# Constant tiles set once, and a value copy that takes only the changing columns, in a fused attention and mixture-of-experts block

## The chip, the cores and the metric

The kernel runs on one core of one Trainium2 chip. Its engines each work through a queue of their own: TensorE (PE in the profile; PEld is its weight load), VectorE (DVE), ScalarE (ACT), GpSimd (POOL) and SyncE (SP), which here only issues DMAs. The metric is device time in microseconds, the median of several runs; lower is better. All data are fp32.

## The reference

One transformer block on a sequence of 2048 rows of 256 numbers: attention with 16 heads of width 16 (keys and values come from a latent of 64), a residual and a layer norm, then 16 experts with the two best per row, a shared expert, a residual and a layer norm.

```python
q = (x @ Wq).reshape(B, S, HEADS, HEAD_DIM).transpose(0, 2, 1, 3)
c_kv = x @ Wkv_down
k = (c_kv @ Wk_up) ...        # 12 of 16 numbers of q and k are rotated (rope)
v = (c_kv @ Wv_up) ...
scores = einsum('bhqd,bhkd->bhqk', qf, kf) * scale       # causal
weights = softmax(scores)
out = einsum('bhqk,bhkd->bhqd', weights, v)
x = layernorm(x + out)
scores = softmax(t @ gate_w.T); weights, indices = top_k(scores, 2)
y = sum over experts e of swiglu(t, w1[e], w3[e], w2[e]) * w_e
x = layernorm(x + y + swiglu(t, sw1, sw3, sw2))
```

## The kernel before

**Layout.** Heads are handled four at a time, in four groups `g`. Each head takes 32 columns (PAD): 16 numbers of the head, then column 16 (ONE), then columns that are zero or copies. The 2048 rows are cut into four chunks `c` of 512 and, for keys and values, into 16 blocks of 128. All four heads of a group share a tile of 128 partitions or 128 columns, and their matmuls use 32 rows or columns of TensorE each.

**Attention.** `prologue(c)` transposes a chunk of x and makes the latent. `project_k`, `project_q` and `project_v` make a group's keys, queries and values; `project_k` ends in a GpSimd sum (L428). Scores are computed twice. A `Maxima` step multiplies queries by keys (tile m) and VectorE takes the row maxima (L485 on the diagonal, L490 elsewhere). When all maxima of `(g, c)` are there, `negated` (L492) reduces them and writes the negative into column ONE of a tile `nm` of 128x512 that is zero elsewhere, and `shift` (L500), two steps later, transposes `nm` on TensorE (tile pn) and adds it to the queries (L508), so that the keys' column of ones carries the negative maximum into the second product. A `Weighted` step multiplies keys by those queries (tile s), ScalarE takes the exponential (L535, tile p), GpSimd masks the diagonal (L539), and TensorE multiplies by the values (tile av). Column ONE of the values is 1, so it collects the sum of the weights. ScalarE copies av out (L566, `more`) and GpSimd adds it to `avs` (L567); in steps without a `Maxima` part VectorE adds it directly (L563).

**The values.** `project_v(g, c)` makes 4 products of 128x128 in two PSUM banks. ScalarE copies each bank's 256 columns into a tile `v` (L453, two copies), out of a pool of six buffers, and GpSimd then sets column ONE of each of 16 head parts to 1 (L457). The padded value weights are zero outside the 16 columns of each head, so the copied padding is zero. There are 16 calls of `project_v` and 16 of `negated`.

**Order.** A list of 180 steps, each a `Maxima` part, a `Weighted` part or both, is written out for all groups, and projections, transposes and ends are put at chosen steps (`put`). TensorE's instructions keep that order. The other engines' queues are ordered by the framework, which takes the instruction of highest priority among those it reckons to be ready by its own estimates of durations; it also places the semaphore waits. `nm` has one buffer: its GpSimd memset (L494) must wait until TensorE has transposed the contents before.

**The rest.** After attention come the norm, the choice of experts, a scatter of rows by GpSimd's indirect DMAs (L278), the blocks of 128 rows per expert, an indirect scatter back (L931), and the combination.

The lines that matter here:

```python
            v = kv.tile([P, CH], F32, tag="v", bufs=6, name=f"v{g}_{c}")
            for a in range(2):
                nc.scalar.copy(
                    v.rearrange("p (b a m) -> p b a m", a=2, m=P)[:, :, a, :],
                    pv[a][:, : 2 * P].rearrange("p (b m) -> p b m", m=P),
                )
            nc.gpsimd.memset(v.rearrange("p (h d) -> p h d", d=PAD)[:, :, ONE : ONE + 1], 1.0)
```

Of the kernel before, what the change touches and what calls it, by code (L numbers as in the profile page):

```python
# [1 line left out]

# [8 lines left out]
F32 = mybir.dt.float32  # L11
# [6 lines left out]
P = 128  # L18
S, E = 2048, 256
H, HD, LAT = 16, 16, 64  # L20
NOPE, RD = 4, 12
G = 4
PAD = 32
LOW = HD + NOPE
ONE = HD
CH = 512
# [21 lines left out]
def block_kernel(  # L48
# [14 lines left out]
    nc = tc.nc  # L63
# [78 lines left out]
    def matmul(*args, **kw):  # L142
        pe(nc.tensor.matmul, *args, **kw)
# [142 lines left out]
    with ExitStack() as att:  # L286
        ap1 = att.enter_context(tc.tile_pool(name="ap1", bufs=1))
        kv = att.enter_context(tc.tile_pool(name="kv", bufs=8))
        wk1 = att.enter_context(tc.tile_pool(name="wk1", bufs=1))
# [102 lines left out]
            out=xg[NEXP * S :, :], in_=blank  # L392
        )

        qs, ks, vs, qa, pm, avs = {}, {}, {}, {}, {}, {}

        def bank(name):
            return ps_sc.tile([P, CH], F32, tag="sc", name=name)
# [41 lines left out]
        def project_v(g, c):  # L440

            pv = [bank(f"pv{g}_{c}_{a}") for a in range(2)]
            for b in range(4):
                a = b % 2
                r = slice(a * LAT, (a + 1) * LAT)
                matmul(
                    pv[a][:, (b // 2) * P : (b // 2 + 1) * P],
                    lhsT=ckv[c][r, b * P : (b + 1) * P],
                    rhs=wvs[r, g * P : (g + 1) * P], start=True, stop=True,
                )  # L450
            v = kv.tile([P, CH], F32, tag="v", bufs=6, name=f"v{g}_{c}")
            for a in range(2):
                nc.scalar.copy(  # L453
                    v.rearrange("p (b a m) -> p b a m", a=2, m=P)[:, :, a, :],
                    pv[a][:, : 2 * P].rearrange("p (b m) -> p b m", m=P),
                )
            nc.gpsimd.memset(v.rearrange("p (h d) -> p h d", d=PAD)[:, :, ONE : ONE + 1], 1.0)  # L457
            vs[g, c] = v

        class Maxima:  # L460
# [29 lines left out]
                        nc.vector.tensor_reduce(to, ps, AX.X, ALU.max)  # L490

        def negated(g, c):  # L492
            nm = wk1.tile([P, 4, 4, PAD], F32, tag="nm", name=f"nm{g}_{c}")
            nc.gpsimd.memset(nm, 0.0)  # L494
            nc.vector.tensor_reduce(
                nm[:, :, :, ONE], pm[g, c][:, :, :, : c + 1], AX.X, ALU.max, negate=True
            )
            return nm
# [96 lines left out]
        def whole_m(g, c):  # L595
            return [(g, c, t, kc) for t in range(4) for kc in range(c)]
# [31 lines left out]
        m = whole_m(1, 3)  # L628
# [5 lines left out]
        for g in range(1, G):  # L634
# [9 lines left out]
            else:  # L644
                m = whole_m(g + 1, 3)
# [25 lines left out]
        for step, what, c in (  # L671
            (1, project_k, 1), (1, project_q, 1), (3, prologue, 2), (4, project_v, 0),
            (6, project_k, 2), (7, prologue, 3), (9, project_v, 1), (9, project_q, 2),
            (14, project_k, 3), (17, project_q, 3), (19, project_v, 2), (32, project_v, 3),
        ):
            if what is prologue:
                put(step, what, c)
            else:
                put(step, what, 0, c)
        for g in range(1, G):  # L680
            i = m_first[g, NCH - 1]
# [5 lines left out]
        for (g, c), i in m_last.items():  # L687
            def late(i=i, g=g, c=c):
                nm = negated(g, c)
                put(i + 2, shift, g, c, nm)  # L690
            put(i, late)
            assert i + 3 <= s_first[g, c]
# [23 lines left out]
        while step < len(steps) or prior or at:  # L716
            m, s = steps[step] if step < len(steps) else (None, None)
            m = m and Maxima(*m)
# [376 lines left out]
```

## Time and profile before

| | |
|---|---|
| Median of 3 runs | 812.88 us (811.92 to 813.79) |
| Profiled execution | 803.1 us, its span 801.1 us |
| Mean granted TensorE clock | 0.993 |
| Attention | about 0 to 594 us of the span |
| Experts and combination | about 594 to 801 us |

The page of the profile gives busy time by engine; the groups give it by line and shape, with the idle time of the engine just before and who ended it; a question about one line or tile tells who waited for it; the timeline lists instructions in order of time. The profiled execution is 1.2% shorter than the median of the timed runs, so differences are worked out in its microseconds and then put on the median.

### The profile page before, as it was taken

What the parts mean: (1) busy time and instruction counts of PE and PEld (TensorE: products, weight loads), DVE (VectorE), ACT (ScalarE), POOL (GpSimd) and SP (SyncE); (2) the same over time, 40 slices, a digit from 0 to 9 for tenths busy, and PEclk for the clock granted to TensorE, in tenths of its full rate; (3) what the DMA queues carried; (4) which work ended last, traced back from release to release, by engine and by line L of the source; (5) the groups of instructions that cost most, each with busy time, mean ns of one, the idle gap of its engine ahead of it and who ended that gap; (6) DMA issues with size and microseconds to landing.
All of it is one profiled execution on the core that took longest, in us unless ns stands there. A gap on an engine that the chain in (4) does not pass through costs nothing. (4 is left out here: it accounts for less than half of the span.)

```text
span 801.1 us, 14999 instructions
## 1 busy us (share of the span) xinstructions
PE 771.5 (96%) x5086; PEld 361.3 (45%) x5086; DVE 547.1 (68%) x1489; ACT 445.0 (56%) x997; POOL 323.0 (40%) x557
## 2 busy tenths in 40 slices
PE   7999999999999999999999999999989899999985
PEld 3443433444333344543334453444336466666543
DVE  2768888887687887777788678788775433333276
ACT  1143646377775786766688668875742033333345
POOL 2032524434355454635455454461661333333300
PEclk9999999999999999999999999999999999999998
DMA  5469999991000000001000000000225322222172
GB/s 147 130 174 327 310 301 304 294 301 54 2 1 1 1 2 1 2 19 37 1 2 2 1 2 2 1 2 2 80 84 141 107 80 86 82 86 70 37 230 85
DMA packets 67378, 71.88 MB, mean 90 GB/s; under 512 B 4736, under 2 KB 61539, under 8 KB 67302
## 3 DMA queue, kind: packets, MB, share of 16 engines
q1 hardware_dynamic: 62286, 61.77, 27.7%
q0 software_dynamic: 3552, 8.43, 3.0%
q10 hardware_dynamic: 1464, 0.72, 0.4%
q8 instruction: 41, 0.67, 0.4%
q14 instruction: 35, 0.29, 0.1%
HBM read 26.44 MB, written 45.78 MB: 90 GB/s over the span
## 5 line engine op out<-in xcount | busy, mean ns | idle before, releaser
L535 ACT ACTIVATE p<-s 128x512 f32<-128x512 f32 (+3 forms) x640 | 292.6, 540 | 128.2 <-PE m L140 79.0
L140 PE MATMUL m<-k,q 32*128 32x512 f32 (+3 forms) x1280 | 303.9, 566 | 0.8 <-DVE rot L423 0.5
L140 PE MATMUL s<-qa,k 32*128 32x512 f32 (+3 forms) x1280 | 279.4, 556 | 1.8 <-DVE avs L563 0.7
L490 DVE TENSOR_REDUCE pm<-m 128x1 f32<-128x512 f32 x384 | 237.5, 681 | 44.4 <-PE m L140 44.0
L567 POOL TENSOR_TENSOR avs<-avs,more 128x512 f32<-128x512 f32 (+3 forms) x125 | 136.7, 1094 | 167.3 <-ACT more L566 163.8
L140 PEld LDWEIGHTS s<-qa,k 32*128 32x128 f32 x1280 | 107.1, 184 | 117.6 <-ACT p L535 67.6
L140 PE MATMUL av<-p,v 128*32 128x512 f32 (+3 forms) x1280 | 154.2, 540 | 1.9 <-DVE base L244 1.2
L140 PEld LDWEIGHTS m<-k,q 32*128 32x128 f32 x1280 | 122.7, 184 | 44.5 <-issue 11.9
L485 DVE CUSTOM_DVE_ANT_0 m<-m,qmask 128x512 f32<-128x512 f32 (+3 forms) x256 | 118.3, 521 | 29.1 <-PE m L140 26.1
L566 ACT COPY more<-av 128x512 f32<-128x512 f32 (+3 forms) x125 | 65.6, 525 | 38.3 <-PE av L140 30.4
L539 POOL TENSOR_SCALAR_AFFINE_SELECT p<-p 128x128 f32<-128x128 f32 x256 | 70.5, 297 | 38.2 <-ACT p L535 36.4
L931 POOL DMA_INDIRECT yg<-yb,to x42 | 41.4, 985 | 88.2 <-ACT yb L923 44.1
L140 PEld LDWEIGHTS av<-p,v 128*32 128x32 f32 x1280 | 27.1, 108 | 104.1 <-ACT p L535 54.2
L140 PE MATMUL ph<-w,xbT 128*128 x168 | 60.3, 482 | 2.4 <-DVE xbT L884 1.7
L903 DVE TENSOR_TENSOR rh<-ru,ph 128x176 f32<-128x176 f32 x42 | 14.2, 338 | 53.7 <-ACT ru L901 53.7
L140 PE MATMUL h<-xT,cs 128*128 128x512 f32 (+1 forms) x96 | 43.6, 599 | 4.9 <-DVE sh L794 2.0
L901 ACT ACTIVATE ru<-ph 128x176 f32<-128x176 f32 x42 | 13.3, 318 | 59.3 <-PE ph L140 59.3
L140 PE MATMUL py<-w2r,hT 88*128 x168 | 43.4, 380 | 0.7 <-ACT hT L910 0.7
L278 POOL DMA_INDIRECT xg<-xr,slot x32 | 31.1, 971 | 31.1 <-issue 19.8
L140 PEld LDWEIGHTS ph<-w,xbT 128*128 128x128 f32 x168 | 28.5, 189 | 20.8 <-issue 11.6
L428 POOL TENSOR_TENSOR k<-rot 128x512 f32<-128x512 f32 x16 | 20.3, 1267 | 42.5 <-DVE rot L426 42.5
L140 PEld LDWEIGHTS py<-w2r,hT 88*128 88x128 f32 x168 | 31.7, 189 | 12.0 <-ACT hT L910 1.2
(147 smaller groups left out, 633.3 us busy)
## 6 DMA issues: line engine op xcount, KB each, us to landing
xg<-hot SPq DMA_DIRECT2D x16, 2064.0 KB
w<-in_w_dram SPq DMA_DIRECT2D x4, 1408.0 KB
xb<-xg SPq DMA_DIRECT2D x42, 129.0 KB
got<-yg SPq DMA_DIRECT2D x8, 512.0 KB
w2r<-in_w_dram SPq DMA_DIRECT2D x2, 1408.0 KB
xr<-in_x_dram SPq DMA_DIRECT2D x4, 512.0 KB
out_dram<-o SPq DMA_DIRECT2D x8, 256.0 KB
cs<-in_rope_dram SPq DMA_DIRECT2D x16, 80.0 KB
```

What stands on the lines that cost most here:

```text
L140: tc.keep_in_program_order(op(*args, **kw))
L278: put = nc.gpsimd.indirect_dma_start(out=xg[:, :], out_offset=bass.IndirectOffsetOnAxis(ap=slot[:, j, i : i + 1], axis=0), in_=xr[c][:, t, ...
L428: nc.gpsimd.tensor_tensor(ks[g, c], tmp[:, 0, :], tmp[:, 1, :], ALU.add)
L485: nc.vector.tensor_tensor_reduce(out=ps[:, :n], in0=ps[:, :n], in1=qmask[:, CH - n :], scale=1.0, scalar=3.0 * NEG, op0=ALU.add, op1=ALU.m ...
L490: nc.vector.tensor_reduce(to, ps, AX.X, ALU.max)
L535: nc.scalar.activation(pr[:, n0:], ps[:, n0:], AF.Exp, scale=SCALE)
L539: nc.gpsimd.affine_select(out=diag, in_=diag, pattern=[[1, P]], base=0, channel_multiplier=-1, compare_op=ALU.is_ge, fill=0.0,)
L566: nc.scalar.copy(more[:, n0:], pv[:, n0:])
L567: nc.gpsimd.tensor_tensor(to, to, more[:, n0:], ALU.add)
L901: nc.scalar.activation(u, ph[:, :INTER], AF.Silu)
L903: nc.vector.tensor_tensor(us[b], u, ph[:, INTER:], ALU.mult)
L931: nc.gpsimd.indirect_dma_start(out=yg[:, :], out_offset=bass.IndirectOffsetOnAxis(ap=to[:, 0:1], axis=0), in_=yb, in_offset=None, bounds_c ...
```

## The change

The tiles for the negated maxima (two, instead of a pool of one buffer) and for the values (six, as many as the pool had) are made once, before the steps begin. GpSimd fills all eight with zeros, and sets column ONE of each of 16 head parts in the six value tiles to 1: 14 memsets, written after the loads and before the first projection. `negated` and `project_v` then take them in a fixed turn. The memset in `negated` and the one in `project_v` go, and ScalarE's two copies in `project_v` take 16 of every 32 columns, 128 elements in each partition instead of 256. TensorE's instructions and their order stay.

```diff
+        turn_nm, turn_v = itertools.count(), itertools.count()
+
+        minus = [ap1.tile([P, 4, 4, PAD], F32, tag=f"nm{i}", name=f"nm{i}") for i in range(2)]
+        room_v = [ap1.tile([P, CH], F32, tag=f"v{i}", name=f"v{i}") for i in range(6)]
+        for t in minus + room_v:
+            nc.gpsimd.memset(t, 0.0)
+        for v in room_v:
+            nc.gpsimd.memset(
+                v.rearrange("p (h d) -> p h d", d=PAD)[:, :, ONE : ONE + 1], 1.0
+            )
...
-            v = kv.tile([P, CH], F32, tag="v", bufs=6, name=f"v{g}_{c}")
+            v = room_v[next(turn_v) % len(room_v)]
             for a in range(2):
                 nc.scalar.copy(
-                    v.rearrange("p (b a m) -> p b a m", a=2, m=P)[:, :, a, :],
-                    pv[a][:, : 2 * P].rearrange("p (b m) -> p b m", m=P),
-                )
-            nc.gpsimd.memset(v.rearrange("p (h d) -> p h d", d=PAD)[:, :, ONE : ONE + 1], 1.0)
+                    v.rearrange("p (b a h d) -> p b a h d", a=2, h=4, d=PAD)[:, :, a, :, :HD],
+                    pv[a][:, : 2 * P].rearrange("p (b h d) -> p b h d", h=4, d=PAD)[:, :, :, :HD],
+                )
...
-            nm = wk1.tile([P, 4, 4, PAD], F32, tag="nm", name=f"nm{g}_{c}")
-            nc.gpsimd.memset(nm, 0.0)
+            nm = minus[next(turn_nm) % 2]
             nc.vector.tensor_reduce(
                 nm[:, :, :, ONE], pm[g, c][:, :, :, : c + 1], AX.X, ALU.max, negate=True
             )
```

## The prediction, made before the result was known

> **What bounds the kernel now.** First the page's busy times, then stretches of time, to see whether one engine alone sets the pace of attention. (Columns of the stretches: length, then busy us and instructions of PE, PEld, DVE, ACT, POOL; granted clock; DMA.)
>
> ```profile
> PE 771.5 (96%) x5086; PEld 361.3 (45%) x5086; DVE 547.1 (68%) x1489; ACT 445.0 (56%) x997; POOL 323.0 (40%) x557
> 260.00:310.00 50.00, 50.00 (x402) 19.68 (x400) 40.01 (x91) 38.69 (x81) 23.91 (x37) 1.00 0.01 1
> 460.00:510.00 50.00, 49.98 (x433) 22.78 (x430) 39.81 (x110) 37.49 (x89) 25.09 (x53) 1.00 0.01 1
> ```
>
> In mid-attention TensorE is never idle at a full clock, DVE is busy for 80%, ACT for 75%, POOL for 50%. A full PE row isn't PE at its peak, so the waits matter: PE's weight loads wait longest for ACT's exponentials (67.6 and 54.2 us in all). The pace is a loop of PE, ACT and DVE through the eight PSUM banks; POOL has room. The change takes work from POOL and a little from ACT, so I ask of each removed instruction who waited for it. The questions about lines 494, 457 and 453 answer (summary rows, then "its engine idle until", then "who waited for it"):
>
> ```profile
> L494 POOL MEMSET nm<- x16: 525/526/529, 8.0 to 530.0; 128x512 f32 x16
>   PE pn L140: 12.9, 10
> L457 POOL MEMSET v<- x16: 123/126/131, 35.2 to 479.8; 128x16 f32 x16
>   ACT v L453: 18.1, 7
>   PEld av L140: 0.8, 1
> L453 ACT COPY v<-pv x32: 372/377/440, 34.5 to 479.3; 128x256 f32<-128x256 f32 x32
>   PEld s L140: 1.9, 4
>   PEld m L140: 1.2, 6
> ```
>
> **Part 1, POOL's 32 memsets.** They are 16 x 0.526 + 16 x 0.126 = 10.4 us of POOL, and POOL stood 12.9 + 18.1 us at their heads with everything behind them held. Were that on the path it would be 41 us. The timeline of POOL says it isn't: nearly every memset is followed by an instruction that had to wait for its own data.
>
> ```profile
> 482.69 0.53 POOL L494 MEMSET nm<- 128x512 f32 x1 [2.79 <-PE pn L140]
> 484.45 0.29 POOL L539 TENSOR_SCALAR_AFFINE_SELECT p<-p 128x128 f32<-128x128 f32 x1 [1.23 <-ACT p L535]
> 324.97 0.13 POOL L457 MEMSET v<- 128x16 f32 x1
> 325.41 0.16 PEld L140 LDWEIGHTS av<-p,v 128*32 128x32 f32 x8 [0.76 <-POOL v L457]
> ```
>
> After the memset at 482.69 POOL waits 1.23 us more for an exponential, so the masks start no sooner without it. Only at 325.41 does PE stand behind a memset: it sat behind a 1.27 us sum although its copies were done by 324.23. PE's weight load waited 0.76 us; PE's previous products covered most of that. So part 1 is worth 0 to 0.8 us, taken as 0.3. What is late next there is the exponential and the `more` copy. The reduction into `nm` (L495) never shows an idle DVE ahead of it, so DVE gains nothing from the memset it no longer needs.
>
> **Part 2, ACT's copies.** Today a pair of copies takes 0.65 us (ACT's timeline, everywhere). For 128 elements the nearest rows are these, of the same engine, from PSUM, contiguous:
>
> ```profile
> L535 ACT ACTIVATE p<-s 128x128 f32<-128x128 f32 x64 | 13.2, 293 | 4.9 <-PE s L140 3.2 <-PE m L140 1.6
> L453 ACT COPY v<-pv 128x256 f32<-128x256 f32 x32 | 10.5, 383 | 8.9 <-PE pv L140 8.8
> L566 ACT COPY more<-av 128x128 f32<-128x128 f32 x13 | 3.8, 290 | 3.2 <-PE av L140 3.2
> ```
>
> A copy falls from 383 to about 290 ns. Four 128-wide exponentials in a row take 0.79 us, a pitch of (0.79 - 0.29)/3 = 0.167 us, so a pair takes 0.29 + 0.167 = 0.46 us: 0.19 us less, 16 x 0.19 = 3.0 us of ACT. On the path: 10 PE loads (4 + 6) were released by a copy of v, 3.1 us of waits. At about one late pair each, 10 x 0.19 = 1.9 us comes through; elsewhere ACT waits for PE after the pair and the time is absorbed. Ends: 0 and 3.0; I take 1.9.
>
> The new copies skip 16 of every 32 columns, which no ACT row shows. On DVE the product at L578 reads such columns of PSUM: 424 ns for 256 elements, against 420 for the contiguous copy at L884. I take no penalty; the upper bound is today's 383 ns, that is no saving.
>
> [...]
>
> **Part 3, the start.** POOL gets 8 x 0.526 + 6 x 0.126 = 5.0 us before the first sum of keys; one memset of 0.53 us there goes.
>
> ```profile
> 3.62 0.55 POOL L131 COPY xr<-number 128x4 f32<-128x4 f32 x4
> 7.00 0.22 POOL L340 COPY wks<-wks 128x48 f32<-128x48 f32 x1 [2.83 <-DMA wks<-in_wk_dram]
> ...
> 7.87 0.22 POOL L345 COPY wqs<-sines 128x48 f32<-128x48 f32 x1
> 8.03 0.53 POOL L494 MEMSET nm<- 128x512 f32 x1
> 15.73 1.27 POOL L428 TENSOR_TENSOR k<-rot 128x512 f32<-128x512 f32 x1 [7.17 <-DVE rot L426]
> ```
>
> If the memsets take the place of the one at 8.03 they end by about 13.1, 2.6 us before the sum's data. If they go first, from 4.17 to 9.2, the weight copies end at about 10.1, and their first matmul runs at 12.25. Cost 0. The cover is 7.17 us of idle POOL; without it, with all 14 queued at 15.73, the sum would end at 22.0 instead of 17.0. The matmul that needs it runs at 19.87 after other PE work, so that costs 2.1 us.
>
> **Part 4, waits.** The fixed turn adds a wait only if a tile comes round while in use. By the list of steps the closest call is the eighth `project_v`: made at step 64, its tile's last reader at step 55; for `nm` a reduction at step 139 against a transpose at 129. Nine steps of about 594/180 = 3.3 us are 30 us: cost 0. Were there a wait, it would stand on ACT with the exponentials behind it, or on DVE with the maxima behind it, and PE would wait for both. Memory after attention may be laid out anew, but the one load there with much data (w2r, issued at 593.65, first used at 641.4) has room. The 200 us behind attention only shift.
>
> **Sum.** -0.3 - 1.9 = -2.2 us: 803.1 becomes 800.9 in the profiled execution, 0.27% less; on the median 812.88 - 2.2 = 810.7.
>
> **Rivals.** *A, slower: the queues are ordered anew.* Durations enter the framework's estimates, and the page shows that a queue isn't in program order: the memset at 8.03 stands before the sum at 15.73, though written after it. If the new order puts the pair of v copies ahead of an exponential that PE is waiting for, ACT delays PE by a new pair, 0.46 us, at that place. There are 16 places: 7.4 us at all, 3.7 at half. It beats the gain from 5 places on (5 x 0.46 = 2.3), and is measurable from 9. Half the places without the gain: 812.88 + 3.7 = 816.6; all of them with it: 810.7 + 7.4 = 818.1. For it: the loads wait in 0.2 to 0.8 us pieces all along, with ACT p as their main releaser, so there is no slack for a worse order. Against it: PE's order is fixed and most ACT instructions have one PE product before them.
>
> *B, the same order effect with the other sign:* half the places gain 0.46: 810.7 - 3.7 = 807.0. With all of the ACT saving and of POOL's 0.8 it is 812.88 - 3.0 - 0.8 - 3.7 = 805.4.
>
> *C, nothing comes through:* every saved copy ends in a wait for PE, as after 13 of the 16 pairs in ACT's timeline (0.2 to 1.3 us until the next exponential in mid-attention). 812.9, or some tenths less.
>
> *D, the memsets at the start are queued late:* +2.1, without the gain 815.0, with it 812.8.
>
> **How the numbers follow.** About 0.2% (1.6 us) is what a measurement of this kernel can tell from no change. Forecast 0.42: 0.34 beyond that, 0.08 within it. A 0.32: 0.28 slower, 0.04 within. B 0.10, faster. C 0.12: 0.10 same, 0.01 each side. D 0.04: half slower, half same. Faster 0.45, same 0.24, slower 0.31. The sign is less sure than the mechanism, for 2.2 us is little beside what an order can move. The range goes from B's 805.4 to A's 818.1; the forecast's own is 809.1 (all of 3.0 + 0.8) to 812.9.
>
> **What would show it.** Right: L453's copies at about 290 ns with 128x128 shapes and pairs of 0.46 us; fewer than 3.1 us of PE loads released by them; POOL busy at about 323.0 - 10.4 + 5.0 = 317.6 us; no POOL wait for pn or v; the first sum of keys still at about 15.7, the first av matmul still at 51.4; attention ending about 2 us before 593.7, and the same 207 us after it. Wrong: copies of 370 ns or more (part 2), the sum of keys later (D), longer waits of PE for ACT p or for POOL p while the copies got shorter (A), or a stretch after attention that changed its length.

## The result and the profile after

The changed kernel takes 811.80 us in the median of 22 runs (809.06 to 814.44), the kernel before 810.91 us (808.82 to 814.82, 22 runs on the same chip). The ratio is 1.0005, with a 95% interval of 0.9993 to 1.0017. On another chip, where both kernels take some 5 us less, it is 1.0002 with 12 and 23 runs (0.9988 to 1.0017). The change can't be seen in the time. The profiled execution took 811.7 us (span 809.5 us) against 803.1 us (801.1 us) before. Most of that difference isn't the change's: a second profile of the changed kernel has a span of 803.0 us, a second one of the kernel before 804.8 us.

The page's busy times after:

```profile
PE 778.5 (96%) x5086; PEld 363.5 (45%) x5086; DVE 547.4 (68%) x1489; ACT 441.4 (55%) x997; POOL 317.2 (39%) x539
```

ACT lost 3.6 us (445.0 before), POOL 5.8 us (323.0 before). TensorE shows 7.0 us more for the same 5086 matmuls; that is the clock (0.981 here) and not work, for a later run of the changed kernel with one instruction more, at a granted clock of 0.993, shows 771.0 us.

The copies of values (line 465 now; rows as before: instructions with their shortest, median and longest duration in ns and the first and last start, then who waited for them):

```profile
L465 ACT COPY v<-pv x32: 266/271/296, 34.2 to 479.5; 128x128 f32<-128x128 f32 x32
L465 ACTq EVENT_SEMAPHORE  x1: 17/17/17, 34.1 to 34.1; - x1
...
  PEld s L141: 2.0, 5
  PEld m L141: 1.2, 6
```

A copy fell from 377 to 271 ns in the median. But the weight loads that "waited for" a copy wait as long as before: 3.2 us now, 3.1 us then. The second row is new. It is one separate wait in ACT's queue, because the first copy now needs POOL's constants as well as TensorE's product: in the trace this row waits for a semaphore that TensorE's matmuls raise and the copy itself for one that POOL raises, where the first copy of the kernel before waited for TensorE's alone. Its own 17 ns are nothing; it returns below.

The start, in POOL's timeline:

```profile
8.25 0.99 POOL L401 MEMSET nm<- 128x512 f32 x2
9.18 2.87 POOL L401 MEMSET v<- 128x512 f32 x6
11.98 0.37 POOL L403 MEMSET v<- 128x16 f32 x6
15.60 1.27 POOL L440 TENSOR_TENSOR k<-rot 128x512 f32<-128x512 f32 x1 [3.25 <-DVE rot L438]
```

The fourteen memsets stand behind the weight copies and end 3.25 us before the first sum of keys has its data. The sum begins at 15.60 us (15.73 before).

What the saved ACT time becomes is seen behind a pair of copies. First the kernel before, then the changed one, at the same place (ACT's timeline: start, length, and in brackets the idle time ahead):

```profile
338.11 0.65 ACT L453 COPY v<-pv 128x256 f32<-128x256 f32 x2
338.64 0.81 ACT L535 ACTIVATE p<-s 128x128 f32<-128x128 f32 x4
...
345.43 0.70 ACT L453 COPY v<-pv 128x256 f32<-128x256 f32 x2
346.45 0.60 ACT L535 ACTIVATE p<-s 128x512 f32<-128x512 f32 x1 [0.32 <-PE s L140]
```

```profile
338.34 0.43 ACT L465 COPY v<-pv 128x128 f32<-128x128 f32 x2
338.82 0.79 ACT L545 ACTIVATE p<-s 128x128 f32<-128x128 f32 x4
...
345.49 0.46 ACT L465 COPY v<-pv 128x128 f32<-128x128 f32 x2
346.55 0.60 ACT L545 ACTIVATE p<-s 128x512 f32<-128x512 f32 x1 [0.60 <-PE s L141]
```

At 338 us the exponentials follow the pair without a gap, so a shorter pair lets them start earlier. At 345 us ACT waits for TensorE's product anyway: the wait grows from 0.32 to 0.60 us, and nothing is gained. The first kind occurs at two of the 16 places (338 and 472 us); at the other 14 ACT idles for 0.2 us or more before its next exponential, in the kernel before as in the changed one.

To measure tenths of a microsecond in executions that differ by several, I set the start of the same exponential in two traces beside each other and followed the distance through attention. The next table has the distance to the kernel before, less its value at 168 us; gains and losses are its steps. All these traces run at the full clock between 168 and 525 us.

```
exponential at (us)     215   240   301   343   354   368   407   420   470   484   525
before, again          0.01  0.02  0.03  0.04  0.04  0.04  0.05  0.05  0.07  0.08  0.08
changed                0.00 -0.07 -0.07 -0.28 -0.28 -0.08 -0.07  0.20  0.20  0.00  0.06
changed, again         0.02 -0.05 -0.04 -0.25 -0.25 -0.04 -0.04  0.24  0.25  0.04  0.12
changed, POOL undone   0.02 -0.05 -0.03 -0.24 -0.23 -0.03 -0.01  0.26  0.28  0.07  0.14
changed, copies x2     0.03  0.22  0.24  0.37  0.31  0.38  0.39  0.39  0.41  0.54  0.61
changed, copies x4     0.80  1.68  1.68  2.59  3.19  3.26  3.26  3.26  3.54  4.83  4.91
changed, one more      0.01 -0.05 -0.04 -0.25 -0.24 -0.24 -0.23 -0.23 -0.21 -0.42 -0.35
before, one more       0.02  0.02  0.03  0.04  0.04  0.25  0.25  0.53  0.54  0.55  0.55
```

In the changed kernel two gains of 0.21 us (338 and 472 us) and a small one of 0.07 us at 229 us are there, and two losses of 0.20 and 0.27 us (358 and 413 us) give them back. The experiments ask for the cause of each. (The last run below, with the start's memsets issued four times, isn't in the table; it gives the row of "changed, again" to within 0.01 us.)

### The profile page after: what moved, and what is told of

Same layout as the page of the kernel before. It is cut to its first block, busy times and chain, and to the rows that moved or that the text cites. A ratio compares the mean times of both kernels' runs of the same rounds, so it can differ in the third digit from the quotient of the medians.

```text
span 809.5 us, 14961 instructions
## 1 busy us (share of the span) xinstructions
PE 778.5 (96%) x5086; PEld 363.5 (45%) x5086; DVE 547.4 (68%) x1489; ACT 441.4 (55%) x997; POOL 317.2 (39%) x539
## 5 line engine op out<-in xcount | busy, mean ns | idle before, releaser
L141 PE MATMUL av<-p,v 128*32 128x512 f32 (+3 forms) x1280 | 158.0, 551 | 0.9 <-ACT p L545 0.4
L141 PE MATMUL ph<-w,xbT 128*128 x168 | 62.0, 494 | 2.8 <-DVE xbT L894 1.7
```

Source lines behind the costliest of these rows:

```text
L141: tc.keep_in_program_order(op(*args, **kw))
```

## The experiments

Theory 1: a pair of copies passes its saving on only where no idle time of ACT follows it. Theory 2: more came through, and a lower clock took it back. The forecast's step is the rival of both: 10 of the 16 pairs pass their saving on.

**The kernel before, once more.** No edit.

> The kernel before, unchanged, as a second sample of its clock and of its timeline. Theory 1 (the saved ScalarE time is absorbed): ratio to the kernel before 1.000 +- 0.002; mean granted clock like the changed kernel's 0.979 to 0.989; between half-clock stretches its exponentials keep a constant distance from those of the first profile, with steps of at most 0.3 us. Theory 2 (the 2 us were gained and given back by the clock gate): its clock lies higher than the changed kernel's by about 0.005 (2 us of 810, at half speed), in profile after profile.

It took 806.36 us (12 runs) beside 806.41 us (23 runs) of itself: ratio 0.9997 (0.9977 to 1.0018). Its profiled execution, then that of the changed kernel (span and mean granted clock):

```profile
core 0: 804.8 us, clock 0.983
```

```profile
core 0: 809.5 us, clock 0.981
```

The kernel before shows the low clock too. In the later runs of both kernels side by side (23 and 12, see below) the mean granted clock is 0.986 for both, and the table, taken at full clock, has no 2 us gained. So theory 2 falls. The 0.993 of its first profile was an unusually undisturbed execution: there two stretches of 3.4 us ran at half clock before the last few us, in the changed kernel's profile four of 3.4 us and two of 6.8 us. Two of those (from 573 and 587 us) lie at the end of attention, where the two traces move apart by some 5 us. Of that, 2.9 us appear at 571 us, just ahead of the first of the two; no other trace here has that step, and its cause stays open.

**The copies issued four times.** `for a in range(2)` of line 464 becomes

```
for a in 4 * [0, 1]:
```

> The changed kernel with each pair of copies of v issued four times: about 0.96 us (6 x 0.16) more of ScalarE at each of 16 places, 15 us in all. Theory 1: only what exceeds ScalarE's idle time behind the pair comes through. By the changed kernel's timeline that is 0.28 + 0.34 + 0.55 + 0.34 + 0.96 + 0.36 + 0.34 + 0.96 + 0.36 = 4.5 us: +0.55%. The forecast's step (10 of 16 pairs come through): +9.6 us, +1.2%. All on the path: +15 us, +1.9%.

812.81 us (6 runs), ratio 1.0086 (1.0055 to 1.0118). In the table it ends 4.9 us above the kernel before and the changed kernel alike, against 4.2 us that theory 1 forecast for the 12 places of this stretch. The forecast's step gave 9.6 us and every pair on the path 15 us for all 16 places, which is some 7 and 11 us for these 12. The pair at the place of 338 us:

```profile
342.63 1.45 ACT L465 COPY v<-pv 128x128 f32<-128x128 f32 x8
343.94 0.84 ACT L545 ACTIVATE p<-s 128x128 f32<-128x128 f32 x4
```

With a pair longer by 1.02 us the waits of loads for a copy grow from 3.2 to 5.4 us only. Theory 1 holds in the main, but not alone. Set beside the run with one more instruction (below), which lacks the two losses, this one ends 5.3 us later, about 1 us more than forecast. The excess of 0.3 to 0.5 us each lies at 191, 229, 345 and 479 us. At 229 us the trace names a second way (TensorE's weight loads):

```profile
233.41 0.46 PEld L141 LDWEIGHTS m<-k,q 32*128 32x128 f32 x4 [0.48 <-ACT v L465]
```

Here the next loads for `m` start only when the long copies (232.07 to 233.52 us) are nearly done: TensorE itself waits for the PSUM bank that the copy frees, and the idle time of ACT behind the pair doesn't absorb that.

**POOL's memsets back.** The constants are set at the start and again at each use:

```
+            nc.gpsimd.memset(v.rearrange("p (h d) -> p h d", d=PAD)[:, :, ONE : ONE + 1], 1.0)
...
+            nc.gpsimd.memset(nm, 0.0)
```

> The changed kernel with the 32 removed GpSimd memsets put back (zeroing the tile of negated maxima in each call, column ONE of v after its copies), 10.4 us of GpSimd, beside the 14 at the start. Theory 1: 0 to +0.3 us, ratio to the kernel before 1.000 +- 0.002, exponentials at a constant distance from the changed kernel's in stretches at full clock. Rival: GpSimd in the way of masks and sums, up to +10 us.

807.61 us (12 runs), ratio 1.0021 (0.9999 to 1.0043). POOL again stands long at the memsets (question about the one of `nm`: its duration, then what POOL sat idle for):

```profile
L506 POOL MEMSET nm<- x16: 524/526/528, 12.0 to 486.1; 128x512 f32 x16
...
  PE pn L141: 17.8, 11
```

Still its row of the table differs from the changed kernel's by 0.08 us at most, over 12 of the 16 places. POOL's part is worth nothing that can be seen there, and the two losses at 358 and 413 us remain, so they aren't POOL's. (By a line through span against granted clock of the runs on this chip, the run stands 0.6 us above the kernel before, plus or minus 0.7.)

**The copies issued twice.** `for a in 2 * [0, 1]:` in line 464.

> The changed kernel with each pair of copies of v issued twice: about 0.32 us more of ScalarE at each of 16 places, 5.1 us in all, read from the profile as the distance of its exponentials from the changed kernel's between half-clock stretches. Theory 1: +0.32 us at the two places where exponentials follow the pair without idle time (about 338 and 472 us), nothing elsewhere: 0.6 us, all but 0.1 us of it in two steps. The forecast's step: 3.2 us in about 10 steps of 0.3.

One run of 806.53 us. Against the changed kernel the two steps that theory 1 forecast are there, 0.34 us each at 338 and 472 us. Two things weren't forecast. One is a third such step, 0.27 us at 229 us, where the loads for `m` again start only at the end of the copies (230.13 us, copies from 229.37 to 230.14 us). The other is that the losses at 358 and 413 us are all but gone (0.31 to 0.38 and 0.39 to 0.39 in the table), though the copies got longer. So the losses belong neither to short copies nor to POOL in any plain way.

**Where the losses come from.** At both places the product that the exponential waits for is done, in both kernels, at the same time after the instruction ahead (here the first place; ACT's timeline of the kernel before, then of the changed one):

```profile
356.13 0.59 ACT L566 COPY more<-av 128x512 f32<-128x512 f32 x1 [0.48 <-PE av L140]
357.72 0.60 ACT L535 ACTIVATE p<-s 128x512 f32<-128x512 f32 x1 [1.00 <-PE m L140]
```

```profile
356.16 0.59 ACT L576 COPY more<-av 128x512 f32<-128x512 f32 x1 [0.48 <-PE av L141]
358.02 0.60 ACT L545 ACTIVATE p<-s 128x512 f32<-128x512 f32 x1 [1.28 <-PE m L141]
```

The trace also records the waits in ACT's queue as instructions. The record of the wait ahead of this exponential, 17 ns long, starts 1.53 us after the copy's start in both kernels (at 357.69 us in the changed one). Before, the exponential starts 0.06 us behind it; in the changed kernel, 0.34 us. I numbered all records of ACT and listed each gap of that kind. In the changed kernel they lie at the numbers 575, 703, 831 and 959; in the kernel before at 319 and 447. All are 63 plus a multiple of 128, counted from 0. The changed kernel has 1593 such records, the kernel before 1592: the extra one is the wait at 34.1 us.

Theory 3: ACT pauses for 0.28 us at each 128th record. Mostly it has something queued or is waiting anyway; where the pause falls between a finished wait and the instruction that the wait held back, and TensorE needs that instruction next, it costs its length. One more wait early on moved all later pauses by one place. In the run with the copies issued twice, which has other numbers of waits and copies, only the gap at 575 is left, and its two losses are all but gone with the others.

**The changed kernel again, and with one more instruction.** For the second, the second copy of the very first projection is issued twice:

```
-            for a in range(2):
+            for a in [0, 1, 1][: 3 if (g, c) == (0, 0) else 2]:
```

> The changed kernel once more, beside the kernel before on one chip, so that span and granted clock of every run can be set beside each other: over the 35 runs of the kernel before on the chip of the first experiments the span goes by 464 us for each 1.0 of mean granted clock (so 4.6 us for 0.01), with 0.96 us left over in a single run. Theory 1 (a pair of copies passes its saving on only where the exponential behind it had no idle time: 2 x -0.21 us; and 2 x +0.27 us come back at 350 to 358 and 407 to 413 us): at equal clock the span stands -0.4 to +0.4 us from that of the kernel before. The forecast's step (10 of the 16 pairs pass on 0.19 us, POOL 0.3 us): -2.2 us. POOL's part is worth nothing by both the earlier aligned traces and theory 1.

> The changed kernel with the second copy of values of the very first projection issued twice: one instruction more in ACT's queue, at about 34 us, where ACT waits over 7 us for the next thing, and nothing else. Theory 3, which is new: ACT's records show a gap of 0.34 us in place of 0.06 us between a finished wait and the instruction that it held back, always at the places 63 + n x 128 in the row of ACT's records (after: 575, 703, 831, 959; before: 319, 447), so ACT pauses for some 0.28 us each 128 instructions, and this costs time only where the pause falls between a wait that ended last and its exponential. The changed kernel has one wait more than before on ACT (the first copy of values waits for POOL's constants too), which moves every later pause one place on, at 703 and 831 to such a spot: this is the +0.27 us at 358 and 413 us. With one more instruction the pauses at 703 and 831 fall ahead of the wait, where ACT idles 1.5 us: both gaps are 0.06 us, and the exponentials stand -0.27 us from the changed kernel's behind 358 us and -0.54 us behind 413 us (apart from stretches of half clock); at equal clock the span is 0.5 us shorter than the changed kernel's, 0.1 to 0.9 us shorter than that of the kernel before. Rival (the shorter copies themselves shift ACT against POOL and VectorE, or the waits there are for a buffer): the distance stays within 0.05 us at both places and the gaps stay at 0.34 us.

The changed kernel: 806.07 us (12 runs) beside 806.19 us (23 runs) of the kernel before, ratio 1.0002 (0.9988 to 1.0017). With one more instruction: 805.91 us (12 runs), ratio 1.0005 (0.9988 to 1.0022). A line through span against granted clock of all these runs, with one slope (384 us for 1.0) and a level for each kernel, puts the changed kernel 0.3 us below the kernel before, plus or minus 0.6 us (95%), and the one with one more instruction 0.8 us below, plus or minus 0.6. The forecast's 2.2 us is outside the first interval. Such a line through the runs on the chip of the first four experiments puts the copies issued four times 5.1 us above the kernel before, plus or minus 0.9. (Its slope is 464 us for 1.0 when all kernels there are taken together; the 35 runs of the kernel before alone, for which the expectation names 464, give 450.)

With one more instruction the gaps are gone:

```profile
355.71 0.59 ACT L576 COPY more<-av 128x512 f32<-128x512 f32 x1 [0.48 <-PE av L141]
357.31 0.60 ACT L545 ACTIVATE p<-s 128x512 f32<-128x512 f32 x1 [1.00 <-PE m L141]
```

The table has the rest: no step at 358 and 413 us, both gains kept, and 0.35 us below the kernel before at 525 us. Against the changed kernel's second trace it is 0.47 us, of the 0.54 us forecast. (0.28 us appear at each place; of the first, 0.20 us are left ten us later.) Its profile happens to have its half-clock stretches where the first profile of the kernel before has them (28, 107 and 796 us), so these two spans can be set beside each other as they are: 800.6 against 801.1 us.

**The kernel before with one more instruction.** The same edit in its line 452.

> The kernel before with the second copy of values of the very first projection issued twice: copies, memsets and all else as before, one ACT instruction more at about 34 us. Theory 3 (a pause of 0.28 us in each 128 instructions of ACT): every later pause falls one place on, as in the changed kernel, so that the gaps at records 703 and 831 go from 0.06 to 0.34 us, and the exponentials stand +0.28 us from those of the kernel before behind 358 us and +0.56 us behind 413 us, though nothing of the change is there. Rival (the losses belong to the shorter copies): 0.00 at both places.

One run of 807.07 us. The long copies, POOL's memsets and all else are those of the kernel before, and the gap appears:

```profile
357.26 0.59 ACT L566 COPY more<-av 128x512 f32<-128x512 f32 x1 [0.48 <-PE av L140]
359.13 0.60 ACT L535 ACTIVATE p<-s 128x512 f32<-128x512 f32 x1 [1.28 <-PE m L140]
```

The gaps lie at records 575, 703, 831 and 959 as in the changed kernel, and the exponentials lose 0.21 and 0.28 us at 358 and 413 us. The losses can thus be had without the change, and be taken from it, by one instruction at 34 us. The rival named for these losses, the shorter copies, falls.

**The start's memsets four times.** `for t in 4 * (minus + room_v):` in line 400.

> The eight whole-tile memsets at the start are issued four times: 24 more of them at 0.478 us (2.87 us for six), 11.5 us more of POOL, so the constants are done at about 23.8 us in place of 12.35 us. If the start's memsets are covered as the forecast said (they ended 3.25 us before POOL had its next work, the sum that makes k, at 15.6 us): that sum begins at about 23.9 us and ends at 25.1, the first matmul of m comes at about 25.2 us in place of 19.6 to 21.0 us, and the exponentials behind stand up to 5.3 us later, less what the idle time of TensorE up to 46 us takes up (4 us). If there were no cover and the memsets lay on the path in full (rival D): +11.5 us, and the present set would cost about 3.8 us already. If POOL's work at the start does not matter at all: 0.

POOL's timeline, then TensorE's:

```profile
23.29 1.27 POOL L440 TENSOR_TENSOR k<-rot 128x512 f32<-128x512 f32 x1
```

```profile
24.61 3.37 PE L141 MATMUL m<-k,q 32*128 32x512 f32 x16 [3.46 <-POOL v L403]
```

The sum of keys begins at 23.3 us and the first matmul of `m` at 24.6 us, against 21.0 us in the changed kernel's first trace and 19.6 us in that with the copies issued four times. So 11.5 us of memsets cost 3.6 to 5.0 us at this point, and the present set lies wholly under the cover. The run (a single one) took 810.03 us; at equal clock it lies 1.9 us above the kernel before, plus or minus 1.8, so how much of the delay reaches the end isn't settled.

## Why the prediction was right or wrong, by its own steps

The time lay in the range, and the sign was open as forecast; the likeliest case, 2.2 us saved, is not what happened. Rival C is, to which the forecast gave a chance of 0.12: nearly every saved copy ends in a wait for TensorE. The range, 805.4 to 818.1 us, has room for a gain, a loss and no change alike. That the measured 811.8 us lies near the forecast's 810.7 us is luck: the forecast set out from the 812.88 us of three runs, and the median of 22 runs of the kernel before is 810.91 us.

*Part 1, POOL, taken as 0.3 us:* at most 0.1 us. The reading that the masks start no sooner without the memset was right. The one weight load that waited 0.76 us for a memset, at 325 us, leaves no step in the table between 301 us and the gain at 338 us: it was covered in full, not in most.

*Part 2, durations:* right. 290 ns were forecast for a copy and 272 measured in the mean, 0.46 us for a pair and 0.43 measured, 3.0 us less of ACT and 3.6 measured. The forecast took no penalty for copies that skip 16 of every 32 columns, and none is seen: runs of 16 columns out of 32 take 272 ns for 128 elements, where the contiguous 128-wide copy took 290 before.

*Part 2, the path:* the step that failed. Ten weight loads named a copy as what released them, 3.1 us in all, and from this 1.9 us were taken as coming through. Copies shorter by 28% left those waits at 3.2 us. Here such a wait says which instruction freed a bank last, and mostly not that TensorE was late for it. At one place, 229 us, TensorE was late for it; there the shorter pair gave 0.14 us, of which 0.07 us are left beside a loss of 0.07 us just ahead. What passed a saving on is mainly read behind the pair: the idle time of ACT before its next exponential. It was zero at two of 16 places, and these two gave 0.21 us each. So some 0.5 us came through in place of 1.9. The text of rival C had that very reading (13 of 16 pairs end in a wait), which leaves three pairs at most; the sum should have used it.

*Part 4, waits:* that the fixed turn makes nobody wait was right. But the change did add a wait, the one at 34.1 us. Its duration costs nothing; its place in ACT's queue shifted the pauses behind it, and 0.47 us went to two of them. No part of the forecast had such a term, and the trace of before had shown it only as gaps of 0.34 us at two harmless places.

*Part 3, the start:* right in time and order; rival D is out. The cover was quantified rightly too: the sum forecast from four sets of memsets came out within 0.6 us.

*Rivals A and B:* on VectorE, ACT, POOL and SyncE the order of instructions in the trace is that of before but for the memsets taken out and put in; TensorE's is written out in the program. Neither case occurred.

*The sum as measured, attention from 168 to 525 us:* two gains of 0.21, the 0.07 at 229 us, two losses of 0.20 and 0.27, and some hundredths give +0.06 to +0.12 us. The forecast that attention would end 2 us earlier in the profile failed for this and for the half-clock stretches of that execution; between two single profiles, the span says nothing about a change of this size.

*The better version:* the changed kernel with one more ACT instruction keeps both gains and has no loss at 358 and 413 us. Its median can't be told from that of either kernel; only the aligned traces and the comparison at equal clock put it ahead of the kernel before, by 0.35 us over that stretch and 0.8 us in all (plus or minus 0.6).

## What to carry to other kernels

Here a saving on ACT reached the end mainly where ACT went on at once with something that TensorE needed (two of 16 places, 0.21 us each): count the places where no idle time follows the shortened work, not the waits that name it as releaser; of those waits only the ones that hold the bound engine up count, here at one place (229 us, 0.14 us). When two profiles differ by more than the change can explain, set the same instruction of both beside each other through the trace and read the steps, and compare timed runs at equal granted clock. One wait more at 34 us moved the pauses behind it in ACT's queue by one place and cost 0.47 us at 358 and 413 us; differences of some tenths of a microsecond far from an edit may be only that.

## What the runs showed of the hardware

**A pause in the instruction stream.** ACT's queue has a pause of 0.28 us at records 128 apart. It is visible where it falls between a finished wait and its instruction (0.34 us in place of 0.06 us): at 319 and 447 in the kernel before, at 575, 703, 831 and 959 in the changed one. In the ten traces together, 18 gaps of 0.34 to 0.36 us stand behind waits that ended after all earlier work of ACT, and all 18 are at places 63 + n x 128; some 90 other such waits in each trace are followed by their instruction within 0.08 us. That the places go by the count of records is shown by the two kernels with one more instruction: at 358 and 413 us the idle time ahead of the exponential falls from 1.28 to 1.00 us in the one and grows from 1.00 to 1.28 us in the other. The page of the changed kernel has two rows that would fit instructions loaded in pieces (packets, MB, share):

```profile
q8 instruction: 41, 0.67, 0.4%
q14 instruction: 35, 0.29, 0.1%
```

The packets of q14 have 8,192 bytes each, and the records of ACT, VectorE, POOL and SyncE (1593, 1661, 777 and 380) make 34.5 pieces of 128. Those of q8 have 16,384 bytes, and TensorE's 10,550 records make 41.2 pieces of 256. The trace also has the start of each packet. Behind each of the four gaps of the changed kernel a packet of q14 starts 0.64 to 0.68 us after the delayed instruction (358.70 us for the exponential at 358.02 us). With one more instruction, where the pause falls into the idle time ahead of the wait, the packet comes earlier too, at 355.71 us, 1.6 us ahead of that exponential (357.31 us). So the pause goes with a packet of q14, by size and count a piece of 128 records. That ACT pauses for the loading of that piece is the likely reading; no run changed the loading.

**Stretches of half clock.** Each profile has two to six stretches, before the last ten us, in which the granted clock is 0.5, always 3.41 or 6.83 us long, with TensorE busy for 73 to 100% of them. Their cause isn't shown: in the changed kernel's first profile TensorE was busy for only 34% of the 3.4 us ahead of the stretch at 645 us, but all the time ahead of those at 157 and 587 us. They come at a few recurring places (near 17, 28, 50, 74, 107, 157, 573, 640 and 766 us above all), some in one execution and others in the next. Most of the spread of single runs goes with them: 0.01 of mean clock goes with 3.8 us of span in the one set of experiments and 4.6 us in the other.
